# First rows of a cross-conditioned mixture-of-experts layer: new order of the work ahead of the first scores, and all first loads on one DMA queue

## The chip, the cores and the metric

The kernel runs on one core of one Trainium2 chip. The metric is the device time of one execution in microseconds. The kernel before takes 462.26 us, the median of 4 runs that lie between 462.18 and 462.37 us. All data is float32.

## The reference

`x` has 8 batch rows of 512 tokens with 256 channels; each batch row has 64 context rows and one condition row of 256 channels. What is computed, cut to what matters here:

```python
nx = layer_norm(x) * ln_gamma + ln_beta
q, k, v = nx @ Wq, context @ Wk, context @ Wv
weights = softmax(q @ k.T / sqrt(256))          # over the 64 context rows
evidence = weights @ v
combined = concat(nx, evidence, cond)           # 768 wide
probs = softmax(combined @ router_W + router_b) # 3 experts
h = silu(combined @ e_w1 + e_b1)                # 3 experts x 512
routed = sum(probs * (h @ e_w2 + e_b2))
g = sigmoid(silu(combined @ gate_w1 + gate_b1) @ gate_w2 + gate_b2)
out = x + g * (routed @ out_w + out_b)
```

## The kernel before, in words

The eight batch rows are taken in four pairs `j` of two rows. For each pair TensorE does the gate's first layer (`gate_layer`), three expert layers (`expert_layer`) and the output products (`outputs`). Products of a pair are joined by a scheme of sums and differences (seven products for a two by two block), which needs `combine_x`: T1 = b12 - b11, T2 = b22 - T1, T3 = b22 - b12 and T4 = b21 - T2, where b12 is the first half of the second row's `nxT`. Before, T3 overwrites b12 and T4 has a place of its own in tile `T`.

The change is in the part that comes ahead of pair 0 and runs once. The order there is written out by hand (L1200 to L1261, under `tc.manual_schedule`): each engine does its instructions in the order of those calls, and the framework adds the semaphore waits. In that order TensorE does:

- 7 matmuls on zeros (`wake`, L294), which start before any data is there
- transposes of the context: half 0, one `wake` matmul, half 1 (`context_transposes`, L311); each half is 256 of the 512 context rows and is copied from PSUM to `ctxT` by one instruction, on VectorE for half 0 and on ScalarE for half 1
- transposes of `Wk` and `Wq` (L326), copied by ScalarE
- values `v = Wv.T ctxT` in two halves of the output channels, 512 columns each (`project`, L335), with the joined keys `wkq = Wk Wq.T` (`join_keys`, L347, one bank, one copy) between them
- small transposes of the biases and the condition (L297, copied by VectorE)
- transposes of the normalised row 0 (`transpose_x`, L574), and the product of joined keys and context `m` (L339 again) in two halves; `keep_m` (L358, VectorE) takes column 0 of each group off the others and puts them into `mr`
- the router's anchor (L374), transposes of row 1, value weights of the gate (`value_weights(0, E)`, L762), the scores of pair 0 (L642), value weights of expert 0, the anchor rows (L432), and then the first gate product (L889)

Beside it VectorE does the layer norm statistics of rows 0 and 1 (L540), `normalize` (L553), one half of each row's scaling after the transposes (`scale_x`, L564; the other half is ScalarE's), T1 and T2, and after the scores the softmax steps up to `turn_weights` (L692), which writes `wT` for the evidence products.

A DMA that SP or ScalarE issues uses one of 8 semaphores in turn, so that every ninth one waits until the one eight places ahead of it has landed. PSUM banks 1, 2, 0 and 3 are handed out in turn by `either` (L283), banks 4, 6 and 7 by `misc` (L104).

Of the kernel before, what the change touches and what calls it, by code (L numbers as in the profile page):

```python
# [16 lines left out]
def kernel(  # L17
# [52 lines left out]
    P = 128  # L70
# [91 lines left out]
    def by_k(flat, n):  # L162
# [14 lines left out]
    rw, rw2, m0, rw_all, gamma_all = (  # L177
        scr[:, NL : NL + 3 * KH * E].rearrange("p (k e) -> p k e", e=E),
        scr[:, NL + P : NL + P + KH * TB].rearrange("p (k e) -> p k e", e=TB),
        scr[:, NL + 2 * P : NL + 2 * P + B],  # L180
        scr[:, NL + 4 * P : NL + 4 * P + H * E].rearrange("p (d e) -> p d e", e=E),
        scr[:, NL + 4 * P + H * E : NL + 4 * P + H * E + H],
    )
# [99 lines left out]
    def either(name):  # L283
        turn[0] += 1
        return bank((1, 2, 0, 3)[turn[0] % 4], name)
# [11 lines left out]
    def small_transposes():  # L297
        pt = either("pt_rows")
        nc.tensor.transpose(pt[:, :NR], rows, ident[:NR, :NR])
        nc.vector.tensor_copy(cols, pt[:, :NR])  # L300
        nc.gpsimd.tensor_copy(b2T[:, :, :E], b2_c.rearrange("p e k -> p k e"))
        pt = either("pt_cond")
        for k in range(KH):
            nc.tensor.transpose(
                pt[:, k * B : (k + 1) * B], cond_sb[:, k * P : (k + 1) * P], ident[:B, :B]
            )
        nc.vector.tensor_copy(
            condT[:, :, :B], pt[:, : KH * B].rearrange("p (k b) -> p k b", b=B)
        )

    def context_transposes():  # L311
        for d in range(2):
            if d:
                wake(1)
            pt = either(f"pt_ctx_{d}").rearrange("p (k c) -> p k c", k=KH)
            for k in range(KH):
                for t in range(NX // 2):
                    nc.tensor.transpose(
                        pt[:, k, t * P : (t + 1) * P],
                        ctx_sb[:, d * (NX // 2) + t, k * P : (k + 1) * P],  # L320
                        ident,
                    )
            half = slice(d * NX // 2 * P, (d + 1) * NX // 2 * P)
            (nc.scalar.copy if d else nc.vector.tensor_copy)(ctxT[:, :, half], pt)

    def transpose_weights(dst, w_sb, name):  # L326
        pt = either(f"pt_{name}")
# [13 lines left out]
                )  # L341
            evacuate(m, ps)

    def keep_v(m, ps):
        nc.scalar.copy(vT[:, m, :], ps)

    def join_keys():  # L347

        ps = either("ps_kq").rearrange("p (m n) -> p m n", n=H)
        for m in range(KH):  # L350
            for k in range(KH):
                nc.tensor.matmul(  # L352
                    ps[:, m, :], wkT[:, k, m * P : (m + 1) * P], wqT[:, k, :],
                    start=(k == 0), stop=(k == KH - 1),
                )
        nc.scalar.copy(wkqT, ps)

    def keep_m(m, ps):  # L358
        ps = ps.rearrange("p (b c) -> p b c", c=CT)
        nc.vector.tensor_copy(m0, ps[:, :, 0])  # L360
        nc.vector.tensor_tensor(
            mr[:, m, :, 1:], ps[:, :, 1:], m0.unsqueeze(2).to_broadcast([P, B, CT - 1]), ALU.subtract
        )


# [208 lines left out]
    def transpose_x(b):  # L574
        S["nxT", b] = npool.tile([P, KH, T], F32, tag="nxT", name=f"nxT_{b}")
        for k in range(KH):
            pt = misc(f"pt_x_{b}_{k}")
            for t in range(NT):
                nc.tensor.transpose(  # L579
                    pt[:, t * P : (t + 1) * P], S["xn", b][:, t, k * P : (k + 1) * P], ident  # L580
                )
            scale_x(S["nxT", b][:, k, :], k, pt, k % 2 == 0)

    def logits(j):

# [45 lines left out]
    def combine_x(j, engine, ts=range(4)):  # L631

        b11, b21, b12, b22 = (S["nxT", 2 * j + i][:, k, :] for i in range(2) for k in range(KH))
        if 0 in ts:
            S["T", j] = work.tile([P, 3, T], F32, tag="T", name=f"T_{j}", bufs=1)
        t1, t2, t4 = (S["T", j][:, i, :] for i in range(3))
        t3 = b12
        for i, (dst, p, q) in enumerate(((t1, b12, b11), (t2, b22, t1), (t3, b22, b12), (t4, b21, t2))):
            if i in ts:
                engine.tensor_tensor(dst, p, q, ALU.subtract)  # L640

    def scores(j):  # L642
# [22 lines left out]
        S["sm", j] = sm  # L665
        if j == 0:
            nc.vector.tensor_tensor(w, w, by_token(mx), ALU.subtract)
            nc.scalar.activation(w, w, AF.Exp, scale=SCALE)
            return
        nmx = work.tile([P, NJ], F32, tag="nmx", name=f"nmx_{j}")  # L670
        nc.vector.tensor_scalar_mul(nmx, mx, -SCALE)
# [171 lines left out]
    def nx_product(j, n, which, start=False):  # L843
        q = GROUPS[n]
        c = 2 * q
        A, Bx, T_ = S["nxT", 2 * j], S["nxT", 2 * j + 1], S["T", j]

        def a(k, d):
            return w1[:, k, (c + d) * P : (c + d + 1) * P]

        dst, lhsT, rhs = {
            1: (U, a(0, 0), A[:, 0, :]),
            2: (Y, a(1, 0), A[:, 1, :]),
            3: (Z, ws[:, S4, q, :], Bx[:, 1, :]),
            4: (U, a(1, 1), T_[:, 2, :]),
            5: (Z, ws[:, S1, q, :], T_[:, 0, :]),
            6: (U, ws[:, S2, q, :], T_[:, 1, :]),
            7: (U, a(0, 1), Bx[:, 0, :]),
        }[which]
        product(dst[n], lhsT, rhs, start=start)  # L860

# [337 lines left out]

    with tc.manual_schedule(engines=None):  # L1200
        ctx_rows = context.flatten_outer_dims().rearrange("(t p) d -> p t d", p=P)
        for d in range(2):
            half = slice(d * NX // 2, (d + 1) * NX // 2)
            nc.sync.dma_start(ctx_sb[:, half, :], ctx_rows[:, half, :])
        for w_sb, w in ((wk_sb, Wk), (wq_sb, Wq)):
            nc.scalar.dma_start(w_sb, rows_of(w))
        nc.sync.dma_start(wv_sb, rows_of(Wv))
        load_table(AF.Sqrt)
        load_x(0)
        load_x(1)  # L1210
        for g in (E, 0):
            load_first(g)
# [2 lines left out]
            load_first(g)  # L1215

        wake(7)
        context_transposes()
        transpose_weights(wkT, wk_sb, "wk")
        transpose_weights(wqT, wq_sb, "wq")  # L1220
        statistics(0, 0, NT)
        deviation(0, 0)
        normalize(0)
        project(wv_sb, ctxT, keep_v, "v", (0,))
        join_keys()
        project(wv_sb, ctxT, keep_v, "v", (1,))
        statistics(1, 0, NT // 2)
        small_transposes()
        statistics(1, NT // 2, NT)
        transpose_x(0)  # L1230
        deviation(0, 1)
        load_router_column()
        normalize(1)
        load_table(AF.Exp)
        project(wkqT, ctxT, keep_m, "m")
        router_anchor()
        transpose_x(1)
        value_weights(0, E)
        store_router_rows(0)
        store_router_anchor()  # L1240
        combine_weights(E)
        combine_x(0, nc.vector, (0, 1))
        scores(0)
        router_column()
        spread_router_bias()
        combine_weights(0)
        spread_router_rows(0)
        value_weights(0, 0, nc.scalar.copy, False)
        anchor_rows(E)
        anchor_rows(0)  # L1250
        sum_weights(0)
        softmax(0)
        value_differences(0, 0)
        combine_x(0, nc.vector, (2,))
        turn_weights(0)
        late_scratch()
        load_anchor(1)
# [123 lines left out]
```

## Time and profile before

| What | Value |
|---|---|
| Median of 4 runs | 462.26 us (462.18 to 462.37) |
| The profiled execution | 462.34 us |
| Its span, first to last instruction | 460.6 us |
| Granted TensorE clock over the span | 1.000 |
| TensorE (PE) busy | 455.2 us, 1455 matmuls |
| VectorE (DVE), ScalarE (ACT), GpSimd (POOL) busy | 365.2, 214.7 and 100.3 us |
| First transpose of real data starts | 4.60 us |
| Scores of pair 0 start | 19.87 us |
| First gate product starts | 24.44 us |

The profile is one execution; its times count from the start of the span. PE is TensorE's matmuls, PEld its weight loads, SPq and ACTq the instructions with which SP and ScalarE issue DMAs. A float32 matmul appears as two records, and a matmul record's time has the drain of the array in it, so that records overlap: the distance of their starts is what a matmul costs TensorE. A line of the timeline gives the start, the time, engine, source line, operation, tiles and shapes and, in brackets, the idle time of the engine before it and what ended that. The loads of the first microseconds, with issue and landing (issue time plus the time to landing that the profile gives):

| Load | KB | Issued by | Issue, us | Landed, us |
|---|---|---|---|---|
| Wk | 256 | ScalarE | 0.74 | 4.7 |
| context half 0 | 256 | SP | 0.74 | 4.4 |
| context half 1 | 256 | SP | 1.24 | 5.9 |
| Wq | 256 | ScalarE | 1.26 | 6.3 |
| Wv | 256 | SP | 1.74 | 7.0 |
| x row 0 | 512 | SP | 2.25 | 8.6 |
| x row 1 | 512 | SP | 2.76 | 10.3 |

### The profile page before, as it was taken

The numbers are of one execution on the slowest core, as the hardware profiler recorded it, in microseconds if no ns is written. First come the engines' busy times: TensorE is split into PE (matmuls) and PEld (weight loads), VectorE is DVE, ScalarE is ACT, GpSimd is POOL, SyncE is SP. The second block draws the span as 40 slices with busy tenths as digits, with TensorE's granted clock in tenths as the row PEclk, the third lists the DMA queues.
The fourth block names the chain that finished last, engine by engine and source line by source line (L and its number), as shares of the span: only waits on it lengthen the run. The fifth ranks groups of instructions, "written<-read, shape, count | busy, mean of one in ns | idle before, by whom it ended". The sixth has DMA issues, their size and how long they took to land.

```text
span 460.6 us, 4752 instructions
## 1 busy us (share of the span) xinstructions
PE 455.2 (99%) x1455; PEld 209.2 (45%) x1455; DVE 365.2 (79%) x683; ACT 214.7 (47%) x370; POOL 100.3 (22%) x149
## 2 busy tenths in 40 slices
PE   8999999999999999999999999999999999999997
PEld 6544555444444444444444444444444444444445
DVE  2888979969799669869799659878889624797983
ACT  3445683655222666557221576448231455458000
POOL 6447715001181300001072300001062300000010
PEclk9999999999999999999999999999999999999999
DMA  8975577302013326812011234602011480000004
GB/s 275 369 158 132 100 232 126 83 0 46 7 23 46 77 86 139 153 28 46 6 24 28 41 137 114 110 7 46 6 24 23 74 203 0 0 0 1 0 14 78
DMA packets 119401, 35.27 MB, mean 77 GB/s; under 512 B 106044, under 2 KB 116336, under 8 KB 118864
## 3 DMA queue, kind: packets, MB, share of 16 engines
q1 hardware_dynamic: 115312, 27.02, 28.8%
q0 software_dynamic: 2176, 7.17, 4.5%
q10 hardware_dynamic: 1888, 0.79, 0.6%
q8 instruction: 11, 0.18, 0.2%
q14 instruction: 14, 0.11, 0.1%
HBM read 27.56 MB, written 7.39 MB: 76 GB/s over the span
## 4 chain that ended last, share of the span: by engine, by line
PE 98%; DMA 1%; DVE 0%; SPq 0%; issue 0%
PE ps_u L796 45%; PE ps_z L796 20%; PE ps_y L796 14%; PE ps_vw L771 5%; PE ps_gu L796 3%; PE ps_w2o L501 2%; PE ps_s L649 2%; PE ps_gz L796 1%; PE ps_tokens L796 1%; DMA scr_ctx<-in_ctx_dram 1%; PE ps_v L339 1%; PE ps_m L339 1%; PE ps_gy L796 1%; PE ps_ar L440 0%; PE ps_kq L352 0%; PE pt_x L579 0%
## 5 line engine op out<-in xcount | busy, mean ns | idle before, releaser
L880 DVE TENSOR_TENSOR h<-h,pb 128x512 f32<-128x512 f32 x96 | 61.9, 694 | 6.5 <-ACT h L829 6.5
L796 PE MATMUL ps_u<-h,w2o 128*128 128x512 f32 x144 | 64.2, 595 | 0.0
L829 ACT ACTIVATE h<-h,abias 128x512 f32<-128x512 f32 x72 | 49.6, 719 | 13.4 <-DVE h L835 12.9
L796 PE MATMUL ps_u<-nxT,w 128*128 128x512 f32 x112 | 55.3, 604 | 0.0
L796 PE MATMUL ps_z<-wT,vw 64*128 64x512 f32 x104 | 49.5, 605 | 0.0
L1105 POOL TENSOR_TENSOR yb<-yb,xb 128x512 f32<-128x512 f32 x14 | 17.7, 1267 | 141.9 <-DVE yb L1104 127.2
L796 PE MATMUL ps_z<-h,w2s 128*128 128x512 f32 x96 | 42.5, 592 | 0.0
L796 PEld LDWEIGHTS ps_u<-h,w2o 128*128 128x128 f32 x144 | 27.0, 190 | 32.6 <-issue 29.4
L838 ACT COPY h<-ps_u 128x512 f32<-128x512 f32 x48 | 28.0, 583 | 29.4 <-PE ps_u L796 27.0
L415 POOL DMA_DIRECT2D vrd<-vw x8 | 5.0, 629 | 136.8 <-ACT vw L778 136.8
L1072 DVE TENSOR_TENSOR h<-h,h 128x1024 f32<-128x1024 f32 x24 | 34.3, 1482 | 0.0
L796 PEld LDWEIGHTS ps_u<-nxT,w 128*128 128x128 f32 x112 | 20.2, 189 | 29.5 <-issue 24.2
L829 ACT ACTIVATE h<-ps_u,abias 128x512 f32<-128x512 f32 x24 | 16.5, 687 | 29.7 <-PE ps_z L796 29.4
L796 PEld LDWEIGHTS ps_z<-h,w2s 128*128 128x128 f32 x96 | 18.2, 190 | 23.0 <-issue 22.3
L796 PE MATMUL ps_y<-nxT,w 128*128 128x512 f32 x56 | 28.6, 592 | 0.0
L796 PE MATMUL ps_z<-T,ws 128*128 128x512 f32 x56 | 28.6, 592 | 0.0
L835 DVE TENSOR_TENSOR h<-h,ps_y 128x512 f32<-128x512 f32 x24 | 16.4, 682 | 14.8 <-PE ps_y L796 14.0
L796 PE MATMUL ps_u<-wT,vw 64*128 64x512 f32 x56 | 27.8, 611 | 0.0
L796 PE MATMUL ps_y<-wT,vw 64*128 64x512 f32 x56 | 27.0, 596 | 0.0
L771 PE MATMUL ps_vw<-w,vT 128*128 128x512 f32 (+1 forms) x64 | 26.9, 542 | 0.0
L796 PE MATMUL ps_u<-T,w 128*128 128x512 f32 x56 | 26.6, 592 | 0.0
L796 PE MATMUL ps_z<-nxT,ws 128*128 128x512 f32 x56 | 26.6, 592 | 0.0
(229 smaller groups left out, 789.9 us busy)
## 6 DMA issues: line engine op xcount, KB each, us to landing
pb<-pd POOLq DMA_DIRECT2D x4, 1536.0 KB, 6.5
xb<-in_x_dram SPq DMA_DIRECT2D x64, 64.0 KB, 2.6
out_dram<-yb SPq DMA_DIRECT2D x56, 64.0 KB, 2.0
w<-in_L_xcond_e_w_dram SPq DMA_DIRECT2D x6, 512.0 KB, 10.4
x<-in_x_dram SPq DMA_DIRECT2D x24, 128.0 KB, 3.2
xd<-x SPq DMA_DIRECT2D x24, 128.0 KB, 2.4
xg<-xd SPq DMA_DIRECT2D x48, 64.0 KB, 2.5
scr_wa<-in_L_xcond_e_w_dram SPq DMA_DIRECT2D x3, 512.0 KB, 17.3
```

The source lines that it names most:

```text
L339: nc.tensor.matmul(ps, w_sb[:, k, m * P : (m + 1) * P], src[:, k, :], start=(k == 0), stop=(k == KH - 1))
L415: nc.gpsimd.dma_start(S["vrd", j][i].rearrange("e c -> c e"), S["vw", j][row_half(i), R0:])
L501: nc.tensor.matmul(ps[:, d * H : (d + 1) * H], w2T[:, k, (i + d) * P : (i + d + 1) * P], ow_sb[:, k, :], start=(k == 0), stop=(k == KH - 1),)
L649: nc.tensor.matmul(ps[side(i, h), g * NH : (g + 1) * NH], mr[:, k, 2 * j + i, g * TB : (g + 1) * TB], S["nxT", 2 * j + i][:, k, h * NH : ( ...
L771: nc.tensor.matmul(ps, vT[:, k, j * 2 * CT : (j + 1) * 2 * CT], w1[:, KH + k, n0:n1], start=(k == 0), stop=(k == KH - 1),)
L796: nc.tensor.matmul(ps, lhsT, rhs, start=start, stop=True, skip_group_check=not start)
L829: nc.scalar.activation(h, h if src is None else src, AF.Silu, bias=abias[:, c, 2 * j + i : 2 * j + i + 1])
L835: nc.vector.tensor_tensor(h, h, part, ALU.add)
L838: nc.scalar.copy(chunk(n, i, d), part)
L880: nc.vector.tensor_tensor(h, h, S["pb", j][:, i, :, 2 * q // RC, :], ALU.mult)
L1072: nc.vector.tensor_tensor(d, p, m, ALU.subtract)
L1105: nc.gpsimd.tensor_tensor(yb, yb, S["xb", 2 * j + row][:, i, :], ALU.add)
```

## The change

Loads: `Wk` and `Wq` move from ScalarE's queue to SP's. SP now issues context half 0 in two pieces of 128 KB, `Wv`, context half 1, `Wk`, x row 0, `Wq` and x row 1, in this order, ahead of the first-layer weights.

Order: the values are computed by halves of the context (`values(d)`, 256 columns for both halves of the output channels, in one bank) instead of by halves of the output channels; half 0 comes before the transposes of context half 1. Two more `wake` matmuls stand ahead of it (3 instead of 1). The transposes of `Wq` stand between the two output halves of `values(1)`. `join_keys` is cut into two calls with a bank and a copy each. The two halves of `m` are parted by the transposes of row 0.

Engines: each context half is copied by VectorE (first 128 channels) and ScalarE (the others); `cols` and `condT`, the first columns of `m` (each `m` has now its own) and both halves of row 0's scaling go to ScalarE. The table load for the exponential moves behind the gate's value weights. The copy of expert 0's value weights stands now ahead of the exponential and `value_differences(0, 0)` behind it.

For pair 0, T3 goes to `T`'s third place and is made ahead of the scores; T4 goes to b12.

```diff
 def context_transposes(*ds):
     for d in ds:
...
-            (nc.scalar.copy if d else nc.vector.tensor_copy)(ctxT[:, :, half], pt)
+            nc.vector.tensor_copy(ctxT[:, 0, half], pt[:, 0, :])
+            nc.scalar.copy(ctxT[:, 1, half], pt[:, 1, :])
+    def values(d, step=None):
+        half = slice(d * NX // 2 * P, (d + 1) * NX // 2 * P)
+        ps = either(f"ps_v_{d}").rearrange("p (m c) -> p m c", m=KH)
+        for m in range(KH):
+            for k in range(KH):
+                nc.tensor.matmul(
+                    ps[:, m, :], wv_sb[:, k, m * P : (m + 1) * P], ctxT[:, k, half],
+                    start=(k == 0), stop=(k == KH - 1),
+                )
+            if m == 0 and step:
+                step()
+        nc.scalar.copy(vT[:, :, half], ps)
+    def join_keys(m):
+        ps = either(f"ps_kq_{m}")[:, :H]
...
+        nc.scalar.copy(wkqT[:, m, :], ps)
+    def first_column(m, ps):
+        products[m] = ps.rearrange("p (b c) -> p b c", c=CT)
+        nc.scalar.copy(m0[:, m, :], products[m][:, :, 0])
...
-            scale_x(S["nxT", b][:, k, :], k, pt, k % 2 == 0)
+            scale_x(S["nxT", b][:, k, :], k, pt, k % 2 == 0 and b > 0)
...
+        if j == 0:
+            t3, t4 = t4, t3
...
-        for w_sb, w in ((wk_sb, Wk), (wq_sb, Wq)):
-            nc.scalar.dma_start(w_sb, rows_of(w))
+        for t in range(NX // 2):
+            nc.sync.dma_start(ctx_sb[:, t : t + 1, :], ctx_rows[:, t : t + 1, :])
         nc.sync.dma_start(wv_sb, rows_of(Wv))
+        nc.sync.dma_start(ctx_sb[:, halves[1], :], ctx_rows[:, halves[1], :])
+        nc.sync.dma_start(wk_sb, rows_of(Wk))
         load_table(AF.Sqrt)
         load_x(0)
+        nc.sync.dma_start(wq_sb, rows_of(Wq))
         load_x(1)
...
         wake(7)
-        context_transposes()
+        context_transposes(0)
+        wake(3)
+        values(0)
+        context_transposes(1)
         transpose_weights(wkT, wk_sb, "wk")
-        transpose_weights(wqT, wq_sb, "wq")
         statistics(0, 0, NT)
+        values(1, lambda: transpose_weights(wqT, wq_sb, "wq"))
+        join_keys(0)
         deviation(0, 0)
+        statistics(1, 0, NT // 2)
         normalize(0)
-        project(wv_sb, ctxT, keep_v, "v", (0,))
-        join_keys()
-        project(wv_sb, ctxT, keep_v, "v", (1,))
-        statistics(1, 0, NT // 2)
+        join_keys(1)
         small_transposes()
         statistics(1, NT // 2, NT)
+        project(wkqT, ctxT, first_column, "m", (0,))
+        deviation(0, 1)
+        keep_m(0)
         transpose_x(0)
-        deviation(0, 1)
         load_router_column()
         normalize(1)
-        load_table(AF.Exp)
-        project(wkqT, ctxT, keep_m, "m")
+        project(wkqT, ctxT, first_column, "m", (1,))
+        keep_m(1)
         router_anchor()
         transpose_x(1)
         value_weights(0, E)
+        load_table(AF.Exp)
...
-        combine_x(0, nc.vector, (0, 1))
+        combine_x(0, nc.vector, (0, 1, 2))
```

## The prediction, on record before the changed kernel ran

> **What bounds the kernel now.** I read first the page's busy times and its chain, then TensorE's waits, then the timeline of the first 25 us by engine, last the DMA landings.
>
> ```profile
> PE 455.2 (99%) x1455; PEld 209.2 (45%) x1455; DVE 365.2 (79%) x683; ACT 214.7 (47%) x370; POOL 100.3 (22%) x149
> ...
> PE 98%; DMA 1%; DVE 0%; SPq 0%; issue 0%
> ```
>
> The chain that ended last is TensorE at 98%, so a microsecond counts only if it is one of TensorE's. TensorE's waits, whole run (who, for whom, us in total, times, longest):
>
> ```profile
> PE ps_wake L294 <- DVE warm_t L186: 1.1, 1, 1.1
> PE pt_ctx L318 <- DMA scr_ctx<-in_ctx_dram: 0.7, 2, 0.5
> PE ps_s L649 <- DVE nxT L566: 0.2, 1, 0.2
> ```
>
> There is nothing else: after the scores start at 19.87 us TensorE never waits until the end. So the change is worth just what it moves the start of the scores, and its ceiling is what TensorE loses ahead of them. Its timeline there (start, us):
>
> ```profile
> 1.06 3.36 PE L294 MATMUL ps_wake<-scr_small 128*128 128x128 f32 x14 [1.06 <-DVE warm_t L186]
> 4.60 0.70 PE L318 MATMUL pt_ctx<-ident,scr_ctx 128*128 128x128 f32 x4 [0.19 <-DMA scr_ctx<-in_ctx_dram]
> 5.14 0.39 PE L294 MATMUL ps_wake<-scr_small 128*128 128x128 f32 x2
> 6.02 0.65 PE L318 MATMUL pt_ctx<-ident,scr_ctx 128*128 128x128 f32 x4 [0.49 <-DMA scr_ctx<-in_ctx_dram]
> 6.51 0.60 PE L330 MATMUL pt_wk<-ident,scr_w 128*128 128x128 f32 x4
> 6.95 0.60 PE L330 MATMUL pt_wq<-ident,scr_w 128*128 128x128 f32 x4
> 7.38 1.95 PE L339 MATMUL ps_v<-scr_ctx,scr_w 128*128 128x512 f32 x4
> 9.17 1.89 PE L352 MATMUL ps_kq<-scr_w,scr_k 128*128 128x256 f32 x8
> ...
> 18.65 1.04 PE L771 MATMUL ps_vw<-w,vT 128*128 128x258 f32 x4
> 19.87 1.93 PE L649 MATMUL ps_s<-nxT,mr 128*32 128x256 f32 x32 [0.19 <-DVE nxT L566]
> ```
>
> The starts give the costs: four transposes 0.44, `ps_v`'s half 1.79 us, `ps_kq` 1.72. From 6.02 to 19.87 are 13.85 us. The last wait in it: `ps_vw`'s four records are 0.22 apart, so TensorE was free at 18.65 + 4 x 0.22 = 19.53 and stood 0.34 for `nxT`. **The work from context half 1 to the scores is thus 13.5 us**, and the change keeps all of it: values, keys and `m` have the same columns in another order.
>
> **The change on TensorE: scores = start of the values + 13.5 + what it waits or loses.** Before: 6.02 (context half 1 is the first of the 13.5) + 13.5 + 0.34.
>
> Start of the values after. The 14 zero records are 0.21 apart, so TensorE is free at about 4.21. The data: added up over both queues, the landings are 512 KB at 4.7, 768 at 5.9, 1024 at 6.3, 1280 at 7.0, 1792 at 8.6 and 2304 at 10.3. If the engines serve bytes in order whichever queue holds them, the new order lands context half 0 (256 KB) at about 4.0, `Wv` (512) at 4.7, context half 1 (768) by 5.9, `Wk` 6.3, row 0 (1536) 7.8, `Wq` (1792) 8.6, row 1 10.3. The ends for half 0 are 4.0 and the 4.4 seen with a rival queue; I take 4.0, as the rows that follow show full bandwidth (352 GB/s at 8.0 to 8.5 us) on one queue alone.
>
> So the four transposes start at 4.21, three of them at the slow pitch of 0.21 that the zero records show, and end with the drain at 5.1. Then the copies. No row has a 128x256 copy on VectorE; its ends are 0.16 (L300, 28 columns) and 0.69 (L324, 512), and a straight line gives 0.42; ScalarE's is 0.38 (L778, 258 columns).
>
> ```profile
> 5.34 0.69 DVE L324 COPY scr_ctx<-pt_ctx 128x512 f32<-128x512 f32 x1 [4.33 <-PE pt_ctx L318]
> ...
> 13.80 0.16 DVE L300 COPY cols<-pt_rows 128x28 f32<-128x28 f32 x1
> ```
>
> The built program's waits hold a surprise: ScalarE's copy of the second 128 channels waits for VectorE's copy of the first, not for TensorE; both read one bank. They go in turn: channels 0 to 127 are ready at 5.1 + 0.04 + 0.42 = 5.56, the others at 5.98. The first value matmul takes only the first, its two passes last 0.43, so the second hides. The three added `wake`s (6 x 0.11) fill 4.92 to 5.58. **The values start at 5.61.**
>
> New wait: `values(1)` behind context half 1. Half 0's values end at 5.61 + 1.79 = 7.40, the transposes at 7.84 (drained 8.01), VectorE's copy at 8.47, so its first matmul starts at 8.52; only `Wk`'s transposes (to 8.28) stand between. **0.24 lost.** Before, the transposes of both `Wk` and `Wq` (0.87) covered a 0.59 copy. Queued behind it is all of TensorE. `Wq` is wanted at 9.46 and lands at 8.6: 0.9 spare.
>
> Switching: a first `ps_v` record takes 0.66 instead of 0.59, so each restart behind transposes costs 0.07, and there are two or three more; with the way back to transposes **0.2**, ends 0 and 0.3.
>
> Keys: `Wq`'s copy ends at 10.7, `join_keys(0)` is due at 10.85. The copies of both key parts (0.38) hide behind the other part, the small transposes and `m`'s first pass (0.43 a record).
>
> The wait for `nxT` (0.34) goes. What is late next? VectorE's row: deviation 0 sits behind the first key copy on ScalarE, which starts when those keys are drained at 11.9, so at about 12.2; then 0.3 + 0.2 + 1.3 (`normalize`) + 1.07 (two statistics) + 0.65 (`keep_m`) + 1.5 (`normalize` of row 1) = 17.3, for transposes of row 1 due at 17.7. `keep_m(1)` and the scaling (0.6 + 0.8) then end `nxT` at 19.2, for scores due at 19.55. Both have over 0.3 spare, so I cost this wait at nothing; gone its cover, it costs what it is late.
>
> Sum: 5.61 + 13.5 + 0.24 + 0.2 = **19.55, against 19.87: 0.3 us earlier.**
>
> **What costs nothing, and what hides it.** ScalarE takes two small copies, two first columns (about 0.2) and one more scaling (0.78), 1.5 us in all, between 12 and 17 us, where it idled over 4 us before. The exponential's table load (1.28) now follows 20.1 and ends by 21.6; the next copy, of expert 0's value weights, is due at 23.5. T3 (0.69) stands ahead of the scores' end; T3 and `value_differences` (0.42) leave the chain from scores to `wT`, which ended at 30.5 for evidence at 31.5 and now ends at about 29. TensorE didn't wait there, so this 1.1 us buys nothing. SP issues three transfers more (0.4 to 0.5 each), so row 1 is issued at about 4.0 instead of 2.76; its data is due at 10.3. The weights behind them keep their place by bytes; the first in use, the gate's, is wanted at about 18. GpSimd's queue keeps its order, and its last small load ahead of the bias transposes needs only to be in by 12.6. T4 in b12 comes after all its readers.
>
> **Two rules of the Trainium skill.** The row first: context half 1, issued 0.5 us behind half 0 on the same queue, landed 1.5 us after it, and `Wv`, issued 0.5 us later still, 1.1 us after that: issues overlap. "DMA: Bandwidth & Descriptors" (Anatomy of one DMA) puts a fixed cost of about 2.0 us on each DMA, for GpSimd's path, and its Bandwidth section asks for transfers of 1 MiB, which speaks against the split of half 0. Were that cost serial, the second piece would land about 2 us later and the sum become about 1.3 us slower (an estimate from that page); these rows speak against it. And the pitch of the zero records, 0.21, falls to 0.11 within the first context transposes; "TensorE: Matmul & The Clock Gate" (Part 1) says that about 3.4 us of activity release the clock, in a window that runs free. By it, transposes started 0.4 us sooner are cold for longer, as counted above, and the earlier start buys little.
>
> **The rivals.**
> 1. *Full cover*: the copies start per half of a bank, or switching is free; 0.24 and 0.2 vanish and the scores start at 19.11. 462.34 - 0.76 = 461.6. For it: the work is there to fill. Against: the waits as built.
> 2. *One queue is too slow* (the other side). If SP's queue brings bytes no faster than its own share did (512 KB at 5.9, 1792 at 10.3), `Wv` lands at 5.9 and the values start at 6.0 (+0.4), and `Wq` lands at 10.3 for a want of 9.87 (+0.4): 19.55 + 0.8 = 20.35, 0.5 us later than before. 462.34 + 0.5 = 462.8. It decides from `Wv` later than 5.56 or `Wq` later than 9.4; together 0.3 us late they eat the gain. Against: on its own, later, this queue shows the full rate.
> 3. *The gain is lost behind the scores.* TensorE gets to the evidence 0.3 us sooner while `wT` waits: 462.34. Against: `wT` comes 1.5 us sooner.
>
> **How the numbers follow.** From the profiled execution, 462.34 - 0.3 = 462.04 (span 460.3 and the same 1.7 around it). It lies 0.08 above the median of the four runs, so the forecast is 461.96. Measured differences below about 0.2% (0.92 us) can't be told from no change with certainty. Chances: the forecast, with a gain of 0 to 0.6 us, 0.60; full cover 0.16; slow queue 0.15; gain lost 0.04; something not seen 0.05. Faster by over 0.2% (below 461.34) needs more than all that TensorE loses (0.76) and has 0.06, from the tail of full cover and the unseen; slower by over 0.2% (above 463.18), lateness of 1.2 us in all, has 0.08, from the tail of the slow queue and the unseen; same 0.86. The range runs from full cover, less a little for the two bounds of half 0's landing, to the slow queue: 461.45 to 462.85.
>
> **What would show it.** Right: values near 5.6 us, a wait of 0.2 on `ps_v` for VectorE's copy of `scr_ctx`, no wait on `ps_s`, scores near 19.55, no TensorE wait after. Wrong: context half 0 later than 4.2, `Wq` later than 9.4, a wait on the transposes of row 1 for `normalize`, or the clock granted later than 4.8 us.

## The result, and the profile after

The changed kernel takes **463.16 us** (median of 30 runs, 462.37 to 463.93); the kernel before takes 462.34 us on the same chips (48 runs, 462.09 to 462.74). The ratio is **1.0018, 95% interval [1.0013, 1.0023]**: 0.8 us slower, and outside the predicted range of 461.45 to 462.85. The profiled execution took 463.37 us, its span is 461.4 us.

TensorE's waits in the changed kernel, whole run (who, for whom, us in total, times, longest):

```profile
PE ps_wake L294 <- DVE warm_t L186: 1.1, 1, 1.1
PE pt_wq L327 <- DMA scr_w<-in_L_xcond_Wq_dram: 0.5, 1, 0.5
```

The waits for the context's loads and for `nxT` are gone, as predicted. One new wait has come: the transposes of `Wq` wait for their load. Behind the scores TensorE again waits for nothing. The timeline of TensorE's matmuls ahead of the scores (start and time in us; in brackets the idle time before the group):

```profile
4.21 1.06 PE L314 MATMUL pt_ctx<-ident,scr_ctx 128*128 128x128 f32 x4
5.06 1.16 PE L294 MATMUL ps_wake<-scr_small 128*128 128x128 f32 x6
6.06 1.89 PE L347 MATMUL ps_v<-scr_ctx,scr_w 128*128 128x256 f32 x8
...
8.23 0.60 PE L327 MATMUL pt_wk<-ident,scr_w 128*128 128x128 f32 x4
8.91 1.13 PE L347 MATMUL ps_v<-scr_ctx,scr_w 128*128 128x256 f32 x4
10.54 0.63 PE L327 MATMUL pt_wq<-ident,scr_w 128*128 128x128 f32 x4 [0.50 <-DMA scr_w<-in_L_xcond_Wq_dram]
...
20.72 1.93 PE L662 MATMUL ps_s<-nxT,mr 128*32 128x256 f32 x32
```

Read it by the starts; the distance of two neighbouring starts is called the pitch here. The first transposes start at 4.21 as predicted, but they last to 5.06, 0.21 each: half speed for all four, and for the first wakes too. So the values start at **6.06, not 5.61**: 0.45 late. Then `ps_v`'s second record group starts at 8.91, 0.25 behind the end of `Wk`'s transposes (8.23 + 4 x 0.107): that is the predicted wait of 0.24 for VectorE's copy. Last, `pt_wq` is due at 9.87, when the records of `ps_v` ahead of it are through, and starts at 10.54, **0.67 late** (the brackets say 0.50, since a record's time has its drain in it). 19.55 + 0.45 + 0.67 = 20.67, and the scores start at 20.72. These two are nearly all of it: the scores are 0.85 later than in the profile before, where they started at 19.87. The two executions differ by 1.03 us; their spans differ by 0.8, and the other 0.2 lies outside the span.

Why `Wq` is late shows in the DMA's rate. Windows of 1 us (stretch, length, then the busy times of TensorE, its weight loads, VectorE, ScalarE and GpSimd, the granted clock, the DMA engines' busy share and GB/s; the share adds up the times of all packets, so it can pass 1), here before the change:

```profile
5.00:6.00 1.00, 0.53 (x5) 0.34 (x3) 0.66 (x1) 0.00 (x0) 0.79 (x2) 1.00 1.10 356
6.00:7.00 1.00, 0.98 (x9) 0.99 (x10) 0.04 (x1) 0.29 (x1) 0.22 (x1) 1.00 1.11 343
```

And of the changed kernel:

```profile
5.00:6.00 1.00, 1.00 (x8) 1.00 (x7) 0.42 (x1) 0.24 (x1) 1.00 (x3) 1.00 0.84 193
6.00:7.00 1.00, 1.00 (x8) 0.90 (x7) 0.00 (x0) 0.13 (x1) 1.00 (x2) 1.00 0.91 244
```

From 3 to 9 us the kernel before moves 342 to 386 GB/s in every window, the changed one 193 to 330. Its loads land (last of their 16 pieces) at 2.9 and 3.5 (context half 0), 4.84 (`Wv`), 5.59, 7.23 (`Wk`), 9.77 (x row 0), 10.40 (`Wq`) and 12.39 us. The 16 pieces of one load are also further apart: `Wk`'s land between 5.90 and 7.23, row 0's between 7.60 and 9.77, where before row 0's lay between 8.25 and 8.60.

One caution on the clock column: it prints 1.00 until the trace's first clock record, so the release, the step from half to full clock, is read off the pitch of the matmuls (0.21, then 0.11), or off the first record of the trace itself. By it the clock was released at 4.78 us in the profile before, which the prediction took over as 4.8, and at 5.74 us in this one.

### The profile page after: what moved, and what is told of

Read it like the earlier page. It is cut to its first block, busy times and chain, and to the rows that moved or that the text cites. A ratio compares the mean times of both kernels' runs of the same rounds, so it can differ in the third digit from the quotient of the medians.

```text
span 461.4 us, 4778 instructions
## 1 busy us (share of the span) xinstructions
PE 456.4 (99%) x1467; PEld 211.5 (46%) x1467; DVE 365.2 (79%) x679; ACT 216.5 (47%) x377; POOL 100.4 (22%) x149
## 4 chain that ended last, share of the span: by engine, by line
PE 97%; DMA 1%; SPq 1%; DVE 0%; issue 0%
PE ps_u L811 45%; PE ps_z L811 19%; PE ps_y L811 14%; PE ps_vw L786 5%; PE ps_gu L811 3%; PE ps_w2o L512 2%; PE ps_s L662 2%; PE ps_gz L811 1%; DMA scr_w<-in_L_xcond_Wq_dram 1%; PE ps_tokens L811 1%; PE ps_m L336 1%; PE ps_gy L811 1%; PE pt_x L590 0%; PE ps_ar L451 0%; PE ps_kq L359 0%; PE pt_rest L1186 0%
## 5 line engine op out<-in xcount | busy, mean ns | idle before, releaser
L811 PE MATMUL ps_u<-T,ws 128*128 128x512 f32 x56 | 26.6, 592 | 0.0
```

The lines of the kernel that those rows point to most:

```text
L811: nc.tensor.matmul(ps, lhsT, rhs, start=start, stop=True, skip_group_check=not start)
```

## The experiments

All medians are beside runs of the kernel before on the same chip, 461.7 to 463.1 us with medians of 462.26 to 462.41. The table has the numbers of each kernel's profiled execution: when the clock was released, when the scores of pair 0 start, the execution's time, and that time less the scores' start.

| Kernel | Clock released | Scores start | Time | Difference |
|---|---|---|---|---|
| before | 4.78 | 19.87 | 462.34 | 442.47 |
| before again (e12) | 5.72 | 19.41 | 461.82 | 442.41 |
| after | 5.74 | 20.72 | 463.37 | 442.65 |
| after again (e11) | 4.43 | 21.08 | 463.74 | 442.66 |
| e1, new order, old loads | 6.06 | 20.85 | 463.64 | 442.79 |
| e2, Wk and Wq on ScalarE's queue | 6.45 | 20.41 | 463.16 | 442.75 |
| e3, Wq ahead of row 0 | 4.32 | 19.58 | 462.20 | 442.62 |
| e5, e3 with whole half 0 | 5.45 | 19.89 | 462.55 | 442.66 |
| e6, e3 without second wakes | 4.37 | 19.48 | 462.11 | 442.63 |
| e9, two banks | 4.98 | 19.28 | 461.82 | 442.54 |
| e15, e9 with two queues | 7.14 | 20.34 | 462.98 | 442.64 |
| e16, after with two queues | 4.30 | 19.57 | 462.21 | 442.64 |

The last column is the first finding: it is 442.4 to 442.8 whatever the kernel (442.3 to 442.8 over all 20 profiles of this case). **All of the effect is ahead of the scores.** (In this table the kernels in the new order lie about 0.2 above those in the old. That is not TensorE's work behind the scores: from the scores to the end of the span it is 440.6 to 440.8 us in both orders. The 0.2 lies outside the span, and its cause was not traced.)

**The parts of the change alone (e1, e4).** e1 is the new order with the old loads, e4 the old order with the new loads. Each is the changed kernel or the one before with the block of `dma_start` calls exchanged.

> The new order with the loads of before (Wk and Wq on ScalarE's queue, context in two halves, then Wv, on SP's). Wv lands third on SP's queue, 7.1 us before. Queue theory (the loss of the change is Wq's late landing on one queue, 10.4 us): Wq lands near 6.3 and TensorE doesn't wait for it, but the first values wait for Wv until 7.1, so scores at 7.1 + 13.5 + 0.4 = 21.0 and about 463.5 us. Clock theory (the loss is that the first 1.5 us of real work run at half clock): the half clock is over when Wv is in, so the loss would be gone and the time be at or below that of before, 462.3.

> The order of before with the new loads: all on SP's queue, Wq behind x row 0. Before wants Wk at 6.5 and Wq at 6.95. Queue theory: Wk lands at 7.2 and Wq at 10.4, TensorE waits about 3.4 us for it and the time is about 465.7 us. If one queue brought the bytes in order at the full rate (Wq at 8.6) it would be about 464. Clock theory: the idle time of TensorE lets the clock fall or release later, and a part of the loss shows as matmuls at half pitch after 6 us.

e1: 463.81 us (463.45 to 463.98, 6 runs), ratio 1.0031 [1.0019, 1.0042]. In the old loads `Wv` comes last of the weights, and now it is wanted first. This is near the queue theory's 463.5; no time is at or below 462.3, as the clock theory had it. TensorE in e1:

```profile
6.81 1.97 PE L347 MATMUL ps_v<-scr_ctx,scr_w 128*128 128x256 f32 x8 [0.44 <-DMA scr_w<-in_L_xcond_Wv_dram]
```

e4: 467.17 us (466.7 to 467.99, 4 runs), ratio 1.0106 [1.0093, 1.012]. The old order wants `Wk` and `Wq` first, and they now come late. TensorE waits 1.15 and 1.55 us for them, and then something dearer happens, for which the queue theory's 465.7 had no room. Windows of e4:

```profile
8.90:12.00 3.10, 1.91 (x6) 1.40 (x7) 2.09 (x8) 1.02 (x3) 0.00 (x0) 0.50 1.09 309
12.00:15.50 3.50, 3.50 (x7) 1.77 (x6) 2.57 (x9) 0.61 (x2) 1.44 (x6) 0.50 1.06 375
```

The clock column says 0.50: during the second of these waits, at 8.81, the clock fell back, and it stayed at half until 15.64. So neither half of the change stands alone, and in this stretch a wait for a load can cost far more than its own length.

**Where Wq stands, and on which queue (e2, e3).**

```diff
 # e3, against the changed kernel
         nc.sync.dma_start(wk_sb, rows_of(Wk))
+        nc.sync.dma_start(wq_sb, rows_of(Wq))
         load_table(AF.Sqrt)
         load_x(0)
-        nc.sync.dma_start(wq_sb, rows_of(Wq))
 # e2, against the changed kernel
+        for w_sb, w in ((wk_sb, Wk), (wq_sb, Wq)):
+            nc.scalar.dma_start(w_sb, rows_of(w))
...
-        nc.sync.dma_start(wk_sb, rows_of(Wk))
...
-        nc.sync.dma_start(wq_sb, rows_of(Wq))
```

> As changed, but Wk and Wq stay on ScalarE's queue; SP has the two context pieces, Wv, context half 1 and x. Queue theory: Wq lands near 6.3, its wait of 0.5 us at 10 us goes; Wv lands between 4.8 and 6.0, so the values start at about 6.1 as in the changed kernel; scores about 20.1 and 462.5 us, 0.6 below the changed kernel. Clock theory: values start at 6.1 for the clock's sake, and taking Wk and Wq off the queue changes nothing: 463.1.

> As changed, but Wq is issued ahead of x row 0 on the one queue. Queue theory: Wq lands near 8.5 to 9, ahead of its want at 10, the wait of 0.5 us goes; x row 0 lands near 10.4, its statistics end at 12.7, and VectorE's row still meets the transposes of row 1; scores about 20.1, 462.5 us. If instead row 0's statistics were the tight chain, the scores would wait for nxT and the time stay near 463. Clock theory: 463.1, nothing gained.

e3: 462.55 us (462.14 to 462.91, 11 runs), ratio 1.0005 [0.9996, 1.0014]. One line moved takes 0.6 us off the changed kernel; `Wq` lands at 8.76 and nothing waits for it. Row 0 now lands at 10.01 and nothing waits for that either. Its clock was released at 4.32, and its timeline has the shape that the prediction described:

```profile
4.20 0.67 PE L314 MATMUL pt_ctx<-ident,scr_ctx 128*128 128x128 f32 x4
4.70 0.83 PE L294 MATMUL ps_wake<-scr_small 128*128 128x128 f32 x6
5.38 1.99 PE L347 MATMUL ps_v<-scr_ctx,scr_w 128*128 128x256 f32 x8
```

The four transposes start 0.13 apart on average, the values start at 5.38 (predicted 5.61), and the scores start at 19.58 (predicted 19.55). e2: 463.43 us (463.09 to 464.02, 10 runs), ratio 1.0025 [1.0016, 1.0034], though no load was waited for and `Wq` was in at 5.12. In this execution loads alone can't be the cause: its values start at 6.42, and the clock was released at 6.45. The release had to be a second cause. It isn't all of e2, though: the ten times, 463.09 to 464.02, stay above e3's 462.14 to 462.91. `Wv` landed at 6.01 and context half 1 at 7.62 here, 0.9 and 1.8 later than in e3, and were in time only because the clock was late. That they hold up the executions with an early release is likely, but none of those was traced.

**The same two kernels again (e11, e12).** Both unchanged, for a second pair of release and time each.

> The changed kernel unchanged, for a second pair of clock release and time. Theory: values start at 5.38 plus half of what the release is later than 4.3 (5.74 gave 6.06), scores 14.0 us after them plus the wait for Wq; the scores' start less that of the first profile (20.72) is the difference of the times, within 0.2 us. Rival (the release has no part in it): the time differs from 463.37 without a difference in the pitch of the first transposes and wakes.

> The kernel before unchanged, for a second pair of clock release and time. Theory: TensorE waits for context half 1 until 6.0 us there, so any release up to 6.0 changes the start of the scores (19.87) by no more than 0.1, and only a release behind 6.0 costs more, half of what it is later. Rival: the start of the scores moves with the release as in the changed kernel.

The changed kernel in e11, TensorE:

```profile
8.95 0.66 PE L327 MATMUL pt_wk<-ident,scr_w 128*128 128x128 f32 x4 [1.08 <-DMA scr_w<-in_L_xcond_Wk_dram]
10.89 0.63 PE L327 MATMUL pt_wq<-ident,scr_w 128*128 128x128 f32 x4 [0.42 <-DMA scr_w<-in_L_xcond_Wq_dram]
```

The clock came early (4.43) and the values at 5.44, just as expected, but now `Wk` is late as well: it landed at 8.91 instead of 7.23. Scores and time moved by the same amount (0.36 and 0.37). So the lateness of the loads isn't a constant. The kernel before behaved the other way round in e12: the clock was released 0.94 later than in its first profile, and yet the scores came 0.46 earlier. All its first loads landed 0.4 earlier, among them context half 1, for which TensorE waits, at 5.59 instead of 5.97:

```profile
5.64 0.67 PE L318 MATMUL pt_ctx<-ident,scr_ctx 128*128 128x128 f32 x4
```

In the old order TensorE stands waiting for this load while the clock is still at half, so the release costs it little; that was expected. That the landing of its loads moves the kernel before by 0.5 us from one execution to the next was not.

**What makes the loads slow (e5, e13, e14, e16).** The new loads differ from the old ones in two ways: one queue, and half 0 in two pieces. e5 is e3 without the split. It was fast in time but just as slow in rate (240 to 300 GB/s in four of its windows from 3 to 8 us), while e2 with two queues and the split was slow too (246, 326, 263, 245 and 258 GB/s in the five half microseconds from 4.0 to 6.5). So the kernel before was given one of the two each:

```diff
 # e5, against e3
-        for t in range(NX // 2):
-            nc.sync.dma_start(ctx_sb[:, t : t + 1, :], ctx_rows[:, t : t + 1, :])
+        nc.sync.dma_start(ctx_sb[:, halves[0], :], ctx_rows[:, halves[0], :])
 # e13, against before
-            nc.sync.dma_start(ctx_sb[:, half, :], ctx_rows[:, half, :])
+            pieces = [half] if d else [slice(t, t + 1) for t in range(NX // 2)]
+            for piece in pieces:
+                nc.sync.dma_start(ctx_sb[:, piece, :], ctx_rows[:, piece, :])
 # e14, against before
-            nc.scalar.dma_start(w_sb, rows_of(w))
+            nc.sync.dma_start(w_sb, rows_of(w))
 # e16, against the changed kernel: replaces its loads of context and weights
+        for half in halves:
+            nc.sync.dma_start(ctx_sb[:, half, :], ctx_rows[:, half, :])
+        for w_sb, w in ((wv_sb, Wv), (wk_sb, Wk), (wq_sb, Wq)):
+            nc.scalar.dma_start(w_sb, rows_of(w))
```

> The kernel of e3 (Wq ahead of x row 0, one queue), with context half 0 loaded by one DMA of 256 KB instead of two of 128 KB. Split theory (the two small pieces let the DMA engines run dry and let the small GpSimd loads in between): the rate from 4 to 8 us is back at 340 GB/s or more, as before (343 to 371), where e3 has 263 to 317; x row 0 has landed by 8.8 us instead of 10.0; context half 0 lands near 3.9 instead of 3.2 to 4.0. One-queue theory (a single queue can't keep the engines busy): the rate stays at 230 to 320 and x row 0 lands near 10. Time: no load is waited for in e3, so both say about the time of e3, 462.5 (462.1 to 463.0).

> The kernel before with context half 0 loaded in two pieces of 128 KB and nothing else changed (two queues). If the split is what slows the loads: below 330 GB/s in some of the windows from 4 to 8 us (before: 342 to 386), landings spread by more than 0.9 us, time 462.6 to 463.5. If it is the one queue: the rate stays at 340 or more, and the time at 462.0 to 462.4.

> The kernel before with Wk and Wq issued by SP ahead of Wv, whole halves, one queue, and nothing else changed. If one queue is what slows the loads: windows of 230 to 320 GB/s between 3 and 8 us, Wv near 8 instead of 7.0 and TensorE waiting for it, 463.0 to 464. If it is the split: 340 GB/s or more from 4 us on, landings within 0.3 us of those before, 462.1 to 462.6.

> The changed kernel with only its first loads replaced: both context halves whole and x on SP's queue, Wv, Wk and Wq on ScalarE's. Loads theory: 340 GB/s or more from 3 us on, no wait for Wk or Wq; with the wakes and the wait of 0.24 as they are, values at 5.4 to 6.4 by the clock's release, 462.2 to 463.0, median 462.5. Rival: a load is still waited for, 463 or more.

| Kernel | Queues, half 0 | Median (range, runs) | Ratio |
|---|---|---|---|
| e5 | one, whole | 462.48 (461.85 to 462.69, 11) | 1.0002 [0.9993, 1.0011] |
| e13 | two, split | 462.89 (462.44 to 463.65, 10) | 1.0015 [1.0006, 1.0024] |
| e14 | one, whole | 463.53 (463.25 to 463.81, 6) | 1.0027 [1.0015, 1.0039] |
| e16 | two, whole | 462.66 (462.21 to 463.22, 11) | 1.0008 [0.9999, 1.0017] |

The same two windows in e13:

```profile
5.00:6.00 1.00, 0.57 (x5) 0.38 (x3) 0.61 (x1) 0.00 (x0) 0.79 (x2) 1.00 0.84 192
6.00:7.00 1.00, 0.00 (x0) 0.00 (x0) 0.08 (x1) 0.00 (x0) 0.88 (x1) 1.00 0.85 278
```

In e14:

```profile
5.00:6.00 1.00, 1.00 (x7) 1.00 (x6) 0.69 (x1) 0.00 (x0) 1.00 (x3) 1.00 0.92 235
6.00:7.00 1.00, 1.00 (x8) 0.82 (x7) 0.00 (x0) 0.42 (x1) 1.00 (x2) 1.00 0.77 232
```

And in e16:

```profile
5.00:6.00 1.00, 1.00 (x8) 0.86 (x8) 0.42 (x1) 0.37 (x1) 0.79 (x2) 1.00 1.06 327
6.00:7.00 1.00, 1.00 (x6) 0.90 (x6) 0.00 (x0) 0.00 (x0) 0.32 (x1) 1.00 1.09 357
```

Both theories held, each for its kernel: **the split alone and the one queue alone each slow the loads**. Over the stretch from 3 to 9 us the six profiles with whole halves on two queues (before, e1, e7, e12, e15, e16) have 340 to 356 GB/s, and all 14 others 270 to 316. Single windows overlap: e7 drops to 251 GB/s from 5 to 6 us, and e9, with pieces on one queue, has 324 to 357 from 5 us on. In e13 TensorE waits 1.73 us for context half 1, which lands at 7.25 instead of 5.97; with the two pieces the first half was in no earlier (4.55, before 4.47):

```profile
7.30 0.66 PE L318 MATMUL pt_ctx<-ident,scr_ctx 128*128 128x128 f32 x4 [1.73 <-DMA scr_ctx<-in_ctx_dram]
```

In e14 `Wv` lands at 8.10 instead of 7.06 and row 0 at 9.82 instead of 8.6, and the scores wait 0.56 for `nxT`. The values wait for `Wv`:

```profile
8.24 1.95 PE L339 MATMUL ps_v<-scr_ctx,scr_w 128*128 128x512 f32 x4 [0.65 <-ACT scr_w L333]
```

The brackets name ScalarE's copy of `Wq`'s transposes, which these matmuls don't read; `Wv`'s landing is the wait that is left, 0.14 ahead of the start as in e1. With the loads mended, e16 shows the new order by itself: no TensorE wait for a load but 0.15 us ahead of the first transposes (4.36 instead of 4.21; half 0 lands at 4.23), and still 462.66.

**What the new order costs TensorE (e7, e8).** Both kernels with `wake(45)` in place of `wake(7)`: real work starts when context, x, `Wk`, `Wq` and `Wv` are in and the clock is up.

> The kernel before with 45 instead of 7 wake matmuls at the start, so that every first load has landed and the clock is released before real work begins: its time says what the order costs TensorE without loads and clock. The wakes end at 12.3 us (release at 4.3) to 13.4 us (release at 6.5). Clock theory: the old order then takes 14.2 us from the first transpose to the scores (15.27 in the profile before, less 0.75 of waiting for data and slow pitch and 0.35 for nxT); scores at 27.1, time 469.6 (469.0 to 470.1), and the times now spread over about 1 us, like those of the changed kernel, since the release is exposed. Rival (the release has no part in the spread): the spread stays at 0.3 to 0.6 us.

> The changed kernel with 45 instead of 7 wake matmuls at the start: loads and clock are out of the way. If the new order itself is as good as the old one, and only Wq and the clock cost time, it takes no more than e7 plus 0.2 us. By the rows of the traces it costs TensorE more: from the first transpose to the values 1.07 us (four transposes and six wake records at full pitch), from there to the scores 14.0 to 14.2, with the wait of 0.24 for the copy: 15.1 to 15.3 against 14.2 in the old order, so about 0.9 us above e7, 470.5.

The first rows and the scores in e7, the old order:

```profile
13.72 0.60 PE L318 MATMUL pt_ctx<-ident,scr_ctx 128*128 128x128 f32 x4
14.16 0.39 PE L294 MATMUL ps_wake<-scr_small 128*128 128x128 f32 x2
14.38 0.60 PE L318 MATMUL pt_ctx<-ident,scr_ctx 128*128 128x128 f32 x4
...
27.93 1.93 PE L649 MATMUL ps_s<-nxT,mr 128*32 128x256 f32 x32
```

In e8, the new order:

```profile
13.95 0.60 PE L314 MATMUL pt_ctx<-ident,scr_ctx 128*128 128x128 f32 x4
14.39 0.83 PE L294 MATMUL ps_wake<-scr_small 128*128 128x128 f32 x6
15.07 1.99 PE L347 MATMUL ps_v<-scr_ctx,scr_w 128*128 128x256 f32 x8
...
29.14 1.93 PE L662 MATMUL ps_s<-nxT,mr 128*32 128x256 f32 x32
```

Old order 14.21 us, new order 15.19, for expectations of 14.2 and 15.1 to 15.3: **the new order takes 0.98 us more of TensorE's time**. By the starts of the rows 0.46 are wakes (six records in 0.68 us, where the old order has two in 0.22), 0.24 is the wait for the copy, and 0.28 is what the smaller pieces cost: 0.17 in the joined keys, 0.11 in `m`, 0.08 in the values, less 0.08 elsewhere. The times are 470.61 (470.53 to 470.74) and 471.16 (470.56 to 471.57), 4 runs each, ratios to the kernel before 1.0179 [1.0166, 1.0193] and 1.019 [1.0176, 1.0203]. The medians differ by 0.55 and the intervals overlap, so the 0.98 is read off one profile of each and isn't priced by the times: the 45 wakes end where the clock's release puts them (13.72 and 13.95 here, released at 6.36 and 6.84). Both kernels end later than expected, by 1.0 and 0.7 us. The spread expected of e7, about 1 us, did not show in its four runs; e8's four lie 1.0 us apart.

**What the second wakes are for (e6, e17, e18).** e3 without `wake(3)`; e17 and e18 are the same kernel again.

> The kernel of e3 without the three wake matmuls between the first transposes and the first values. Clock theory (values wait for six wake records at half pitch when the clock is released late): values start when the copies of context half 0 are there, about 5.5 us, whatever the clock; the median falls by 0.2 to 0.4 us against e3, to 462.1 to 462.35. Rival (the pause of 0.5 us that the wakes filled puts the release off, or lets the clock fall back as in e4): 463 or more, with PEclk 0.5 in a later window.

> The kernel of e6 unchanged, to catch one of its slow executions. If the pause of 0.5 us puts the release off or lets the clock fall back: an execution of 463 or more shows matmuls at half pitch for up to 3.4 us behind the first values (8 records of values in 3.6 instead of 1.9 us), 1.7 us at most. If late loads make it: a wait of 1 to 2 us for Wk or Wq in it, at full pitch. A fast execution (462.0 to 462.5) decides nothing.

> The same kernel as e17 with the same expectations: half pitch behind the first values in a slow execution if it is the clock, a wait for Wk or Wq at full pitch if it is a load.

e6: 462.46 us, but in two groups: 7 runs from 462.03 to 462.48 and 5 from 463.09 to 464.53; ratio 1.0018 [1.0005, 1.003]. e17 fell in the first (462.34, clock released at 4.52), e18 in the second (464.54). TensorE in e6's profile, released at 4.37:

```profile
5.41 1.99 PE L347 MATMUL ps_v<-scr_ctx,scr_w 128*128 128x256 f32 x8 [0.52 <-DVE scr_ctx L320]
```

In e18:

```profile
5.79 3.78 PE L347 MATMUL ps_v<-scr_ctx,scr_w 128*128 128x256 f32 x8 [0.52 <-DVE scr_ctx L320]
9.36 1.06 PE L314 MATMUL pt_ctx<-ident,scr_ctx 128*128 128x128 f32 x4
```

The values take 3.78 us instead of 1.99: half speed. The clock was released at 10.43 only, and nothing was waited for but the copy. So the rival held in the one slow execution that was profiled: the pause of 0.52 us, where it falls ahead of the release, puts it off. e15 is the comparison: counted back by 3.41 us from its release, its windows end at 3.72 and 7.14 (e18's at 3.61 and 7.02); TensorE was busy without a pause in the second, and the clock came at its end. Where the pause falls behind the release, as in e6's own profile and e17, it does no harm and the median gains nothing measurable. There the wakes cost nothing either, since TensorE would stand for the copies in their place: the values start at 5.38 in e3, with them, and at 5.41 in e6. What they buy is that the release isn't put off.

**Two banks (e9, e10, e15).** Each half of the channels of a context half gets a bank of its own, and two wakes follow instead of three:

```diff
 # e9, against e3
-            pt = either(f"pt_ctx_{d}").rearrange("p (k c) -> p k c", k=KH)
             for k in range(KH):
+                pt = either(f"pt_ctx_{d}_{k}")[:, : NX // 2 * P]
...
+                (nc.scalar.copy if k else nc.vector.tensor_copy)(ctxT[:, k, half], pt)
-            nc.vector.tensor_copy(ctxT[:, 0, half], pt[:, 0, :])
-            nc.scalar.copy(ctxT[:, 1, half], pt[:, 1, :])
...
-        wake(3)
+        wake(2)
 # e10, against e9
-        wake(7)
+        wake(6)
 # e15: e9 with the loads of e16
```

> The kernel of e3 with a bank for each half of the channels of a context half, so that VectorE's and ScalarE's copies need not follow one another and each starts after two transposes, and with 2 instead of 3 wake matmuls behind them. Theory (what the new order costs TensorE is the wakes, 0.64 us at full pitch, and the wait of 0.24 for VectorE's copy ahead of values(1)): VectorE's copy starts after two of four transposes, so the wait falls from 0.24 to 0.1 or less, and the values of half 0 start 0.2 us earlier at full pitch, 0.43 at half pitch; the median falls by 0.3 to 0.5 us against e3, to 462.0 to 462.25. Rival (the wakes hold the clock, as the times of 464 in e6 say): some times at 463.5 or above, the median no better than e3's 462.5.

> The kernel of e9 with 6 instead of 7 wake matmuls at the start. In e3, e5 and e6 the first transpose starts at 4.2 us, when the wakes end, while its data landed at 2.7 to 4.0. Theory (the start is set by the wakes): everything up to the scores comes 0.2 to 0.43 us earlier unless Wv (4.7 to 5.1) or Wq (8.2 to 8.8) is late, so 461.7 to 462.1. Rival (the wakes set when the clock is released, so that fewer of them put it off): no gain against e9, or times of 463.5 and above.

> The kernel of e9 with whole halves, both halves and x on SP's queue, Wv, Wk and Wq on ScalarE's. Loads theory (the spread of e9, 461.6 to 463.1, comes from late loads): 340 GB/s or more from 3 us on, no wait for a load but for context half 0 until 4.4, values at 5.4 to 5.6, scores at 19.3; all times between 461.6 and 462.4, median 461.9. Rival (the spread comes from the clock's release alone): the same spread as e9, with times up to 463.

e9: 461.99 us (461.59 to 463.1, 11 runs; before 462.27), ratio 1.0002 [0.9993, 1.0011]. e10: 462.23 (461.86 to 462.85, 11), 1.0002 [0.9993, 1.001]. e15: 462.67 (461.87 to 463.21, 11), 1.0007 [0.9998, 1.0016]. The wait ahead of `values(1)` fell from 0.24 to 0.12 (0.1 or less was expected), and e9's best time, 461.59, is the lowest of this case, but no version is faster than the kernel before beyond its interval. e15 was to tell whether e9's spread comes from the loads. Its loads ran at 327 to 369 GB/s from 3 us on and none was waited for, and the spread stayed: the loads theory of the spread fell. The values in e9, with the clock released at 4.98:

```profile
5.47 1.89 PE L346 MATMUL ps_v<-scr_ctx,scr_w 128*128 128x256 f32 x8
7.20 0.60 PE L315 MATMUL pt_ctx<-ident,scr_ctx 128*128 128x128 f32 x4
7.63 0.60 PE L326 MATMUL pt_wk<-ident,scr_w 128*128 128x128 f32 x4
8.19 1.10 PE L346 MATMUL ps_v<-scr_ctx,scr_w 128*128 128x256 f32 x4
```

In e15, with the clock released at 7.14:

```profile
5.91 2.50 PE L346 MATMUL ps_v<-scr_ctx,scr_w 128*128 128x256 f32 x8
8.25 0.60 PE L315 MATMUL pt_ctx<-ident,scr_ctx 128*128 128x128 f32 x4
```

Neither execution waits for a load, and the matmuls are the same. The release is 2.16 us later, the second transposes 1.05, the scores 1.06, the times 1.16: **half a microsecond for each microsecond that the release is late**, since work that runs at half speed until then is half done. The other kernels in which no load is waited for say somewhat less: in e3, e5 and e2 (released at 4.32, 5.45 and 6.45) the scores start at 19.58, 19.89 and 20.41, 0.3 to 0.5 for each microsecond. e10 gained nothing: one wake fewer brings the transposes 0.42 forward (3.78 instead of 4.20), but they run at half speed, and the values start at 5.48 as in e9 (5.47). Its clock was released at 5.40, 0.42 later than e9's, so this pair doesn't price the wake by itself.

## Why the prediction was wrong, point by point

- *"The engines serve bytes in order whichever queue holds them"*, at the rate of the old loads: **failed**. It put `Wq` at 8.6; it landed at 10.40 and 10.76 in the two profiles, where it decided from 9.4 by the prediction's own rival. That rival, the slow queue, is half of what happened: `Wq` landed near its 10.3, but `Wv`, which it had at 5.9, was in at 4.84, and the 0.4 by which it had the values late came from the clock. That its start of the values, 6.0, is near the measured 6.06 is luck. And the queue isn't the only cause: e13 shows that the split does it too. The row which spoke against the rival, full rate on one queue, was of 8.0 to 8.5 us; from 5 to 8 us the changed kernel's one queue moved 193 to 300 GB/s. Its price: e3 takes 0.6 us off the changed kernel by moving `Wq` alone.
- *"Three of them at the slow pitch"*, with the clock released at 4.8: **failed**, by 0.45 us here. The release came between 4.30 and 7.14 in the profiles that the wakes covered. The prediction read it off a single execution and used it as a constant; it named a later clock as a sign of being wrong, but gave it no price and no rival. The old order hides it behind its wait for context half 1, the new one does not.
- *Sum of 19.55*: met in e3, with the release at 4.32 and `Wq` in time: 19.58, and 462.20 us in that execution. In part that is luck: the values start 0.23 sooner than in the sum, as the clock was released sooner, and from there to the scores it takes 14.20 us instead of 13.94.
- *The wait of 0.24*, *the copies of 0.42 and 0.38 in turn*: right (0.25; 0.42 and 0.37, ScalarE's copy waiting for VectorE's). *The wait for `nxT` goes*: right.
- *Switching, 0.2*: somewhat small. From the values to the scores, e3, e16, e2 and e5, which wait for no load there, take 14.20, 14.07, 13.99 and 13.97 us; 13.5 + 0.24 leave 0.23 to 0.46.
- *The 1.1 us taken off the chain to `wT` buy nothing*: right in effect, wrong in size. `wT` ends 10.44 us behind the start of the scores, 10.63 before, so 0.2 came off: T3 left the chain, but `value_differences` still stands in it, for 0.73 us from 25.69 on. TensorE waits for it in neither.
- *All that TensorE loses (0.76)*: that figure is the gain of full cover. The waits ahead of the scores before are 0.19, 0.49 and 0.34, in all 1.02.
- What e7 and e8 add to the reckoning as a whole: with loads and clock out of the way the new order takes 0.98 us more of TensorE's time. The sum has most of this in it (the wakes up to 5.61, the 0.24, the 0.2), but spread over its terms. So the new order lives only from starting earlier, and the earlier start is at half speed.

Of the 0.8 us, 0.4 to 0.6 are then the late loads (the changed kernel against e16 and e3, each set against its own runs of the kernel before), and what is left is the order under the clock as it comes: e5, e3 and e16 lie 0.2 to 0.4 above their runs of the kernel before, and their intervals still hold 1. Why the DMA engines idle while loads are queued, with one queue as with two small pieces, stays open.

## What to carry to other kernels

Before you count a start that moves forward as a gain, ask at which clock the work will run: a wait for data in the first 6 us may be hiding a cold TensorE for nothing, and filling it with early work gains half at best. Read landing times from a profile with the same queues and the same transfer sizes, and put the load that is wanted next ahead of the large one; a sum of bytes over all queues says nothing of a single one. And take the mean of several executions, not one profile, for anything that lies in the first microseconds.

## What the runs showed of the hardware

- The clock's release falls anywhere from 4.30 to 7.14 us with the wakes in place, and at 10.43 in e18. The stretches at full clock are whole multiples of one length: 3.41 us in e4, 453.97 (133 times), 457.39 (134 times) and 464.21 us (136 times) in others. "TensorE: Matmul & The Clock Gate" (Part 1) of the Trainium skill describes such a window of 3.4 us that runs free and doesn't start with the kernel; these numbers agree. The page adds that the ramp is under 1% of a typical kernel and need not be modelled to a count. Here half of the 2.84 us between the earliest and the latest release is 1.4 us or 0.3%, which is more than all that the change could gain.
- One queue was slower than two in the first 8 us: 232 to 357 GB/s from 3 to 8 us in e14 against 342 to 386 before. "DMA: Bandwidth & Descriptors" (Rules for kernel authors) says that spreading DMAs over several issuing engines doesn't help bandwidth, as all use the same 16 engines. In this stretch the measurement says otherwise, and the measurement decides; later, from 9 to 10 us, the changed kernel reaches 371 GB/s on one queue.
- A 256 KB load in two pieces of 128 KB, with nothing else changed, cost 0.6 us (e13) and made the next five loads behind it late by 0.7 to 1.3 us.
- How busy TensorE was in the window of 3.41 us ahead of a change of the clock (ends from the trace's clock record): 3.22 us in the kernel before, and the clock was released at its end; 2.89 in e18, and it was not; all 3.41 in e15, and it was. Once released, a window with 1.53 busy ended in the clock falling back for 6.83 us (e4), one with 1.69 busy did not (e13).
